# Three graph-attention layers: partly filled neighbour columns packed densely in all layers, their sources picked by one-hot products

## The chip, the cores and the metric

The kernel runs on one core of a Trainium2 chip. The metric is the device time of one execution in microseconds, the median of several runs. The engines are named as the profile names them: PE (matmul), DVE (vector), ACT (scalar), POOL (GpSimd, which issues the indirect DMAs here) and SP (which issues the plain DMAs).

## What is computed

A graph of 6250 nodes with 256 features and 100000 directed edges (`src`, `dst`, sorted by `dst`) goes through two GATv2 layers of 4 heads by 64 (with a self edge for every node), a residual and a layer norm, then one GAT layer of 8 heads by 32, a residual and a layer norm. Cut to what matters, one head of each kind of layer:

```python
# GATv2, twice (elu in between); edges include the self loops
xl, xr = x @ Wl, x @ Wr
logit = sum(att * leaky_relu(xl[src] + xr[dst], 0.2))
alpha = softmax of logit over the edges with the same dst
h[n]  = sum over edges with dst == n of alpha * xl[src]  + b
x = layernorm(x + h)
# GAT
Wh = x @ W
e  = leaky_relu(a1 . Wh[src] + a2 . Wh[dst], 0.2)
out[n] = sum of softmax(e) * Wh[src];  x = layernorm(x + out)
```

All arithmetic is in float32. An edge costs one gathered row of 256 numbers (1 KB) in each layer.

## The kernel before

**Plan.** `make_plan` sorts the nodes by degree on the chip and cuts them into 49 blocks of 128, one node to a partition, the fullest first. For each block it leaves in DRAM (`near_d`) a list of sources: column j holds the j-th neighbour of each of the 128 nodes, or a dummy node whose row makes the logit hugely negative. The number of columns of a block is fixed ahead from a model of the degrees (`columns`): 27 for block 0, 25 for block 1, then 24, 23, 22, down to 9 for block 48; 803 in all. The few edges of block 0 beyond 27 columns are handled apart (`find_few`). While DVE and PE work on the plan, POOL issues seven gathers whose result nobody reads (`spare`, L1259).

**Gathers.** `gather_rows` (L1475) fetches one column of one block with one indirect DMA of POOL: 128 rows, one to a partition. The last column of a block is often filled in a few nodes only. Ten such last columns are put into three packs of up to 128 lanes: `pick_rows` copies their list entries into one index column with small DMAs of SP, `gather_pack` (L1451) gathers the pack at once, and `lay_rows` and `lack_rows` (SP) put the lanes and the dummy rows into the block's rows tile. So a layer has 793 + 3 gathers of 128 rows. The lists of a pack's later blocks are fetched early for that, and layer 1 leaves the packs' indices for the other layers.

**Rows.** There are 9 rows tiles of 9 columns. A block's columns and the node's own row are cut into chunks that fit a tile: in layers 1 and 2 block 0 has four chunks, blocks 1 to 17 three, blocks 18 to 48 two.

**Layers 1 and 2** are `layer2(i, ...)`, called twice; all order is written by hand (`tc.manual_schedule`), and each engine runs its instructions in program order. One iteration b of the loop at its end:

- `attend(b)`: for each chunk z = max(g, pr), z times att, and a reduce to the logits (L1841, L1844, L1845, all DVE; the first z of a block is made one iteration ahead, in `first_z`, L1821); then the maximum `top` (L1623), ACT's exp, the denominators, and `first_z(b+1)`, which needs pr of that block (L1930 fills a part of pr first).
- `finish(b-1)`: elu, or residual and layer norm, of the block before.
- `weighted_sum(b)` (L1659): the rows times their weights, the last `few` columns by ACT (`mul`, L1673, four for each column), the others by DVE (L1677), and the sum over the columns in PSUM by PE with identity matmuls (`acc`, L1684). In layer 1 `few` is a third of the S columns, in layer 2 two thirds.
- `fetch(b+2)`: the list or rows of block b+4 (`begins`), the packs and the gathers of block b+2.
- `turns(b+2)`: PE transposes (`pt`), ACT copies to `xT`, PE makes pl and pr of block b+2 and the next layer's tables of block b-1, which SP stores as rows of `xl_d`, `xr_d` or `whs_d`.

PE does all of this in the order given: what fetch or turns issue stands behind the whole of acc(b).

**Layer 3** (L2022 on) has its own loop: gather(b+1), then attend(b) with one add per chunk for the logits (L2056), softmax, and `added_up`, products and one long reduce, all on DVE. PE is idle there.

Of the kernel before, what the change touches and what calls it, by code (L numbers as in the profile page):

```python
# [47 lines left out]
def columns(E, N, NB):  # L48
# [30 lines left out]
    part = {}  # L79
    for b in range(len(EARLY), NB):  # L80
        c = cols[b] - 1
        n = max(8, -(-int(math.ceil(over[c] + 3.5 * sd[c] - P * b)) // 8) * 8)
        if n < P:
            part[b] = n
    packs, taken = [], set()
    for b in sorted(part):
        if b in taken or part[b] > P * 3 // 4:
            continue
        pack, at = [], 0
        for k in range(b, NB):  # L90
            if k in part and k not in taken and at + part[k] <= P:
                pack.append((k, at, part[k]))
                at += part[k]
        if len(pack) > 1:
            packs.append(pack)
            taken.update(k for k, _, _ in pack)
    return cols, low, high, held, packs
# [569 lines left out]
def kernel(  # L667
# [22 lines left out]
    cols, low, high, held, packs = columns(E, N, NB)  # L690
# [7 lines left out]
    node_i = plan.tile([P, NB], I32, name="node_i")  # L698
    fits = plan.tile([P, 1], I32, name="fits")
# [11 lines left out]
    with tc.manual_schedule():  # L711
        make_plan(
            tc, x, src, dst, ((wl1, wr1, att1), (wl2, wr2, att2)), (b1, b2), w3, a3,
            cols, low, high, held, packs, node_i, fits, ident, eps, nobody, att, wc, wh, fixed, xl1_d,
            near_d,
        )
        nc.vector.memset(done, 0)
# [4 lines left out]
    with tc.If(ok != 0):  # L722
        with tc.manual_schedule():
            tile_by_degree(
                tc, x, att1, b1, b2, w3, a3, out, [held] + cols[1:], packs, node_i, near_d, ident, eps, nobody,
                xl1_d, att, wc, wh, fixed, done, wl2, wr2, att2,
            )
# [8 lines left out]
def make_plan(  # L736
    ctx, tc, x, src, dst, layers, biases, w3, a3, cols, low, high, held, packs, node_i, fits, ident, eps,
    nobody, att, wc, wh, fixed, xl1_d, near_d,
# [36 lines left out]
    SPARE = 7  # L775
# [218 lines left out]
    for pack in packs:  # L994
        for b, _, n in pack:
            nc.gpsimd.tensor_scalar(
                most[:, b : b + 1], part_of, float(n), float(cols[b] - 1), op0=OP.is_lt, op1=OP.add
            )
# [260 lines left out]
    spare = one.tile([P, SPARE, LONG], I32, name="spare")  # L1259
    for k in range(SPARE):  # L1260
        nc.gpsimd.indirect_dma_start(
            out=spare[:, k, :], out_offset=None, in_=listed,
            in_offset=bass.IndirectOffsetOnAxis(ap=begin_i[:, k : k + 1], axis=1),
        )
# [12 lines left out]
    counts = one.tile([P, NB], F32, name="counts")  # L1277
# [26 lines left out]
def tile_by_degree(  # L1304
    ctx, tc, x, att1, b1, b2, w3, a3, out, cols, packs, node_i, near_d, ident, eps, nobody,
    xl1_d, att, wc, wh, fixed, done, wl2, wr2, att2,
# [52 lines left out]
    late = consts.tile([P, len(EARLY)], F32, name="late")  # L1359
# [78 lines left out]
    packed = {b: (q, r, n) for q, pack in enumerate(packs) for b, r, n in pack}  # L1438
    opens = {pack[0][0]: q for q, pack in enumerate(packs)}
    shuts = {pack[-1][0]: q for q, pack in enumerate(packs)}  # L1440
    picks = [consts.tile([P, len(packs)], I32, name=f"pick{k}") for k in range(2)]
    for pick in picks:
        nc.gpsimd.memset(pick, NP)
    held_rows = {}

    def pick_rows(q, pick, of):

        for b, r, n in packs[q]:
            nc.sync.dma_start(pick[r : r + n, q : q + 1], of[:n, b, cols[b] - 1 : cols[b]])

    def gather_pack(b, pool, name, pick, table, width):  # L1451
        q = opens[b]
        held_rows[q] = pool.tile([P, RW], F32, name=name)
        nc.gpsimd.indirect_dma_start(
            out=held_rows[q][:, :width], out_offset=None, in_=table,
            in_offset=bass.IndirectOffsetOnAxis(ap=pick[:, q : q + 1], axis=0),
        )

    def lay_rows(b, rows, width):

        q, r, n = packed[b]
        nc.sync.dma_start(rows[-1][:n, rows_at[b], :width], held_rows[q][r : r + n, :width])

    rows_at = {}

    def lack_rows(b, rows, cut, table, width):

        n = packed[b][2]
        rows_at[b] = cut[-1][1] - cut[-1][0] - 1
        nc.sync.dma_start(  # L1470
            rows[-1][n:, rows_at[b], :width],
            bass.AP(tensor=table.tensor, offset=table.offset + NP * width, ap=[[0, P - n], [1, width]]),
        )

    def gather_rows(b, rows, cut, own, table, of, width, j0, j1):  # L1475


        for g, (s0, s1) in zip(rows, cut):
            for j in range(max(s0 - own, j0), min(s1 - own, j1)):
                if j + 1 == cols[b] and b in packed:  # L1480
                    continue
                nc.gpsimd.indirect_dma_start(  # L1482
                    out=g[:, j + own - s0, :width], out_offset=None, in_=table,
                    in_offset=source(of, b, j),
                )
# [84 lines left out]
    def sort_sources(work, ps, b):  # L1570

        n = cols[b]
# [19 lines left out]
        if b + 1 == len(EARLY):  # L1592
            pb = ps.tile([P, b + 1], F32, name="pb", tag="tp")
# [148 lines left out]
    def layer2(i, table, of, width, start, own, finish, follow):  # L1742
# [5 lines left out]
        with ExitStack() as es:  # L1748
# [5 lines left out]
            packp = es.enter_context(tc.tile_pool(name=f"pack{i}", bufs=len(packs)))  # L1754
# [5 lines left out]
            def gather(b):  # L1760
                first = EARLY[b] if b in begun else 0
                rows, cut = begun.pop(b) if first else row_tiles(b, 1)
                if b in opens:
                    gather_pack(b, packp, "pack", picks[i], table, width)
                gather_rows(b, rows, cut, 1, table, of, width, first, cols[b])
                if b in packed:
                    lack_rows(b, rows, cut, table, width)
                    if b in opens:
                        waiting.append(lambda: lay_rows(b, rows, width))
                    else:  # L1770
                        lay_rows(b, rows, width)
# [4 lines left out]
            waiting = []  # L1776
# [6 lines left out]
            def fetch(b):  # L1783
                if b + 2 < NB:
                    begins(b + 2)
                if i == 0 and b + 2 in opens:
                    for k, _, _ in packs[opens[b + 2]]:
                        begins(k)
                if i == 0 and b + 1 in opens:
                    pick_rows(opens[b + 1], picks[0], sources)  # L1790
# [35 lines left out]
            def attend(b):  # L1826
# [8 lines left out]
                for g, (s0, s1) in zip(rows, cut):  # L1835
# [11 lines left out]
                    )  # L1847
                if b == 0:
# [9 lines left out]
                few = min(S // 3, cut[-1][1] - cut[-1][0] - 1) if i == 0 else (2 * S - 2) // 3  # L1858
# [4 lines left out]
                if i == 0:  # L1863
# [3 lines left out]
                    if b in shuts:  # L1867
                        pick_rows(shuts[b], picks[1], spots)
# [15 lines left out]
            if i == 0:  # L1884
                find_few(work, pst)
            gather(0)
# [8 lines left out]
            for b in range(NB):  # L1895
# [6 lines left out]
                if b:  # L1902
                    new()

# [12 lines left out]
                if i == 0 and b == len(EARLY):  # L1917
                    load_last()
                if b + 2 < NB and not ahead(b):
# [102 lines left out]
    layer2(0, xl1_d[:, :], sources, W2 + 1, start1, own1, finish1, begin2)  # L2022
    last_weights()
    layer2(1, xl2_d[:, :], spots, W2, start2, own2, finish2, lambda: begin(0, wh_d, A1))

    with ExitStack() as es:
        packp = es.enter_context(tc.tile_pool(name="pack3", bufs=len(packs)))
        work = es.enter_context(tc.tile_pool(name="work3", bufs=3))
        ps = es.enter_context(tc.tile_pool(name="ps3", bufs=3, space=PSUM))
        state = {}  # L2030

        def gather(b):
            first = EARLY[b] if b in begun else 0
            rows, cut = begun.pop(b) if first else row_tiles(b, 0)
            if b in opens:
# [126 lines left out]
```

## Time and profile before

| | us |
|---|---|
| median of 9 runs | 3807.47 (3797.38 to 3831.42) |
| profiled execution | 3815.2 |
| its span | 3813.4 |
| DVE busy | 2720.6 (71%) |
| POOL busy | 2479.0 (65%) |
| PE busy | 1595.5 (42%) |
| ACT busy | 1330.7 (35%) |
| row gathers of layers 1 and 2, POOL (L1482) | 1549, 946 ns each |
| row gathers of layer 3, POOL (L1482) | 756, 1039 ns each |

One profiled execution gives busy times per engine, the idle time in front of each group of instructions and what ended it. The span is that of the instructions; the execution's own time is a little longer. In lines of waits the columns are the total, the number and the longest; in lines of the timeline they are start, duration, engine, line, operation, tiles out<-in, shape and count, with the idle time before the instruction and its releaser in brackets. "issue" is idle time for which the profile shows no cause.

### The profile page before, as it was taken

What the parts mean: (1) busy time and instruction counts of PE and PEld (TensorE: products, weight loads), DVE (VectorE), ACT (ScalarE), POOL (GpSimd) and SP (SyncE); (2) the same over time, 40 slices, a digit from 0 to 9 for tenths busy, and PEclk for the clock granted to TensorE, in tenths of its full rate; (3) what the DMA queues carried; (4) which work ended last, traced back from release to release, by engine and by line L of the source; (5) the groups of instructions that cost most, each with busy time, mean ns of one, the idle gap of its engine ahead of it and who ended that gap; (6) DMA issues with size and microseconds to landing.
All of it is one profiled execution on the core that took longest, in us unless ns stands there. A gap on an engine that the chain in (4) does not pass through costs nothing.

```text
span 3813.4 us, 25469 instructions
## 1 busy us (share of the span) xinstructions
PE 1595.5 (42%) x5424; PEld 1153.7 (30%) x5424; DVE 2720.6 (71%) x2619; ACT 1330.7 (35%) x5161; POOL 2479.0 (65%) x2585
## 2 busy tenths in 40 slices
PE   8235666566556774466655666664000000000000
PEld 6224454344445552343433444443000000000000
DVE  7638888667677886678866788894777566656665
ACT  3113434333334442456555667773000000000000
POOL 5764666665466655666666666664777777777774
PEclk9667888777778896788877778896555555555555
DMA  8433333333233433333433344442433333333332
GB/s 233 125 89 83 105 105 102 106 98 94 77 103 104 111 101 96 100 104 105 114 102 107 111 116 115 117 118 71 109 107 102 98 96 96 98 97 99 99 100 57
DMA packets 176463, 397.64 MB, mean 104 GB/s; under 512 B 50923, under 2 KB 93955, under 8 KB 176283
## 3 DMA queue, kind: packets, MB, share of 16 engines
q0 software_dynamic: 120608, 336.86, 32.5%
q1 hardware_dynamic: 54680, 57.74, 4.9%
q10 hardware_dynamic: 1012, 1.32, 0.1%
q8 instruction: 48, 0.79, 0.1%
q14 instruction: 115, 0.94, 0.1%
HBM read 354.60 MB, written 40.42 MB: 104 GB/s over the span
## 4 chain that ended last, share of the span: by engine, by line
POOL 16%; issue 16%; ACT 13%; DVE 7%; PE 6%; another core or an unknown queue 5%; DMA 1%; POOLq 0%; DVEq 0%; ACTq 0%
POOL g L1482 15%; ACT g L1673 9%; PE acc L1684 5%; ACT at L1631 1%; DVE weighted L1706 1%; DVE acc_v L1718 1%; POOL out L2086 1%; DVE z L1844 1%; DVE lg L1845 1%; PE pm L1612 1%; DVE part_v L1718 1%; DVE z L1841 1%; DMA g<-whs_d,near_r 1%; DVE g L1677 0%
## 5 line engine op out<-in xcount | busy, mean ns | idle before, releaser
L1482 POOL DMA_INDIRECT g<-xl_d,near_r x1549 | 1465.3, 946 | 826.2 <-issue 486.9
L1684 PE MATMUL acc<-g,ident 128*128 128x256 f32 x3408 | 1085.0, 472 | 807.6 <-issue 332.8
L1684 PEld LDWEIGHTS acc<-g,ident 128*128 128x128 f32 x3408 | 754.8, 234 | 1130.6 <-issue 402.5
L1482 POOL DMA_INDIRECT g<-whs_d,near_r x756 | 785.2, 1039 | 276.1 <-issue 244.5
L1673 ACT ACTIVATE g<-g,by 128x64 f32<-128x64 f32 x3080 | 796.4, 337 | 367.8 <-issue 350.7
L1845 DVE TENSOR_REDUCE lg<-z 128x28 f32<-128x1820 f32 (+4 forms) x234 | 497.4, 2125 | 8.1
L1844 DVE TENSOR_TENSOR z<-z,at 128x1820 f32<-128x1820 f32 (+4 forms) x234 | 496.8, 2123 | 4.7
L1718 DVE TENSOR_REDUCE acc_v<-weighted 128x256 f32<-128x3584 f32 (+10 forms) x47 | 319.0, 6787 | 22.3 <-remote 9.9
L1841 DVE TENSOR_TENSOR z<-g,pr 128x1820 f32<-128x1820 f32 (+3 forms) x138 | 299.6, 2171 | 16.9 <-DMA g<-xl_d,near_r 7.8
L1648 ACT ACTIVATE wt<-lg 128x128 f32<-128x128 f32 (+17 forms) x49 | 14.0, 285 | 801.9 <-DVE lg L1647 269.5
L1677 DVE TENSOR_TENSOR g<-g,at 128x256 f32<-128x256 f32 (+8 forms) x185 | 273.7, 1496 | 3.7 <-DVE at L1644 0.4
L1607 ACT COPY xT<-pt 128x256 f32<-128x256 f32 x147 | 51.8, 373 | 534.7 <-PE pt L1602 280.1
L1706 DVE TENSOR_TENSOR weighted<-g,wt 128x1792 f32<-128x1792 f32 (+4 forms) x111 | 227.1, 2057 | 0.3
L1821 DVE TENSOR_TENSOR z<-g,pr 128x2080 f32<-128x2080 f32 (+4 forms) x96 | 197.9, 2061 | 26.5 <-remote 13.8
L2056 DVE TENSOR_TENSOR lg<-g,s_r 128x56 f32<-128x56 f32 (+4 forms) x111 | 22.6, 213 | 268.3 <-DMA g<-whs_d,near_r 236.1
L1930 DVE MEMSET pr<- 128x4 f32 x49 | 3.0, 62 | 253.9 <-PE pr L1612 110.4
L1631 ACT ACTIVATE at<-lg,top 128x19 f32<-128x19 f32 (+14 forms) x392 | 115.8, 295 | 142.3 <-DVE top L1623 60.3
L1612 PE MATMUL pl<-wcat,xT 128*128 128x260 f32 x196 | 81.8, 559 | 90.5 <-ACT xT L1607 80.0
L1728 DVE BATCH_NORM_STATS2 stats<-acc 128x6 f32<-128x256 f32 x49 | 21.1, 430 | 130.4 <-PE acc L1684 84.7
L1612 PE MATMUL pm<-wcat,xT 128*128 128x260 f32 x392 | 102.7, 408 | 13.1 <-ACT xT L1607 13.1
L1612 PEld LDWEIGHTS pm<-wcat,xT 128*128 128x128 f32 x392 | 81.5, 209 | 28.8 <-ACT xT L1607 13.9
L1638 DVE RECIPROCAL den<-den 128x4 f32<-128x4 f32 x98 | 17.0, 174 | 99.5 <-ACT at L1631 61.1
(276 smaller groups left out, 1801.4 us busy)
## 6 DMA issues: line engine op xcount, KB each, us to landing
g<-xl_d,near_r POOLq DMA_INDIRECT x1549
g<-whs_d,near_r POOLq DMA_INDIRECT x756
whs_d<-row SPq DMA_DIRECT2D x49, 132.0 KB
xl_d<-row SPq DMA_DIRECT2D x49, 130.0 KB
xr_d<-row SPq DMA_DIRECT2D x49, 130.0 KB
two<-xl_d SPq DMA_DIRECT2D x49, 130.0 KB
two<-xr_d SPq DMA_DIRECT2D x49, 130.0 KB
near_d<-x_all SPq DMA_DIRECT2D x7, 896.0 KB
```

What stands on the lines that cost most here:

```text
L1482: nc.gpsimd.indirect_dma_start(out=g[:, j + own - s0, :width], out_offset=None, in_=table, in_offset=source(of, b, j),)
L1612: nc.tensor.matmul(pm, xT[:, c, :], w[:, c, :], start=c == 0, stop=c == 1)
L1631: nc.scalar.activation(wt[:, :, h], lg[:, :S, h], AF.Exp, bias=top[:, h : h + 1], accum_out=den[:, h : h + 1],)
L1673: nc.scalar.mul(g4[:, t, h, :], g4[:, t, h, :], by[:, s0 + t - a0, h : h + 1])
L1677: nc.vector.tensor_mul(g4[:, :m], g4[:, :m], wt[:, s0 : s0 + m, :].unsqueeze(3).to_broadcast([P, m, H, F // H]),)
L1684: nc.tensor.matmul(acc, ident, g4[:, t], start=False, stop=s0 + t == S - 1 and not more)
L1706: nc.vector.tensor_mul(prod[:, s0 - base : s1 - base, :].rearrange("p t (h d) -> p t h d", h=H), g[:, :n, :F].rearrange("p t (h d) -> p t ...
L1718: nc.vector.reduce_sum(part, prod[:, : s1 - base, :].rearrange("p s f -> p f s"), axis=AX.X)
L1821: nc.vector.tensor_max(z, rows[0][:, :n, :W2], xr[:, None, :].to_broadcast([P, n, W2]))
L1841: nc.vector.tensor_max(z, g[:, :n, :W2], xr[:, None, :].to_broadcast([P, n, W2]))
L1844: nc.vector.tensor_mul(z, z, at[:, None, :].to_broadcast([P, n, W2]))
L1845: nc.vector.reduce_sum(lg[:, s0:s1, :], z.rearrange("p t (h d) -> p t h d", h=H2), axis=AX.X)
```

## The change

`columns` no longer packs last columns only. `lanes_of` takes every column that by the model of the degrees is less than 75% filled: 33 columns in 28 of the blocks 1 to 48. All their edges, in the order of block, column and partition, are numbered through, and 128 in a row make a pack: 14 packs, dense to the last. The other 770 columns are gathered as before (`base[b]` of them in block b). Since the fill of a column is known only on the chip, the place at which a column begins in the packs is a value found at run time.

- `find_lanes`, at the start of layer 1: counts the edges of each such column (a compare with the nodes' degrees, a matmul with ones), sums them up, holds the sums within bounds fixed ahead (a breach leads to the slow path that is there for any graph), and leaves for every edge its pack and lane.
- `pick_lanes`: for each column a one-hot matrix of the lanes and one of packs times source; their product by PE, summed in PSUM over the columns at hand, gives the sources of the packs. It is called at the start of layer 1 (lists of blocks 0 to 2), in attend(0), and in layer 1's fetch whenever new lists were begun. The sum is added to `pick_f` by DVE after the first chunk of the next attend.
- `gather_packs`, `keep_packs`: a pack is gathered by POOL and stored to DRAM (`pack_d`). `lay_rows` loads each column from there into its place in the rows tile, from a row offset that SP loads into a register; partitions without an edge get some row, and `shut_lanes` adds a hugely negative number to their logits. `lack_rows` puts dummy rows where a column's upper partitions are never filled.
- `pick_again`, in layer 1: the packs' own indices for the other two layers come back from the stored rows' last column.
- The neighbour lists are begun earlier in layer 1, as far as the packs need them; the `spare` gathers, the old picks and packs are gone; in layer 1 `few` is two fifths of the columns; the pack tiles come from the pool `two` in layers 1 and 3.

The diff, cut to its core:

```diff
+    items, top, base = [], [], list(cols)
+    for b in range(1, NB):
+        size = min(P, N - P * b)
+        for c in range(low, cols[b]):
+            if min(size, over[c] - 3.5 * sd[c] - P * b) < 0.75 * P:
+                base[b] = min(base[b], c)
+                items.append((b, c))
+                top.append(max(8, min(P, -(-math.ceil(over[c] + 3.5 * sd[c] - P * b) // 8) * 8)))
...
-    spare = one.tile([P, SPARE, LONG], I32, name="spare")
-    for k in range(SPARE):
-        nc.gpsimd.indirect_dma_start(
...
+        for k, values in enumerate((lo, hi, [0] + top)):
+            i = 0
+            for j in range(1, len(values) + 1):
+                if j == len(values) or values[j] != values[i]:
+                    nc.vector.memset(bound[:, k, i:j], float(values[i]))
+                    i = j
+        for b, own in items_of.items():
+            nc.vector.tensor_scalar(
+                has[:, own[0] : own[-1] + 1], numbers[:, base[b] : cols[b]], counts[:, b : b + 1],
+                None, op0=OP.is_lt,
+            )
...
+        pk = ps.tile([P, K], F32, name="lane_k", tag="tp")
+        for i in range(first, written[0]):
...
+            hot_l = work.tile([P, P], F32, name="lane_hot", bufs=2)
+            nc.vector.tensor_scalar(hot_l, numbers, lane_in[:, 0, i : i + 1], None, op0=OP.is_equal)
+            given = work.tile([P, K], F32, name="lane_given", bufs=2)
+            nc.vector.tensor_scalar(
+                given, numbers[:, 1 : K + 1], lane_in[:, 1, i : i + 1], lane_in[:, 2, i : i + 1],
+                op0=OP.is_equal, op1=OP.mult,
+            )
+            nc.tensor.matmul(pk, hot_l, given, start=i == first, stop=i + 1 == written[0])
...
+        def add():
+            nc.vector.tensor_add(pick_f, pick_f, pk)
...
+    def keep_packs(b, k):
+        for q in packs_at.get(b, ()):
+            nc.sync.dma_start(pack_d[k][q * P : (q + 1) * P, :], held_rows[q][:, : wide[k]])
...
+            nc.sync.dma_start(g[: top[i], j - s0, : wide[k]], pack_d[k][lane(i), :])
...
+    def shut_lanes(b, lg, own, H):
+        if b in items_of:
...
+            nc.vector.tensor_add(s, s, shut[:, i0 : i0 + n].unsqueeze(2).to_broadcast([P, n, H]))
...
+                if i == 0 and b > 1:
+                    pick_lanes(work, pst, begun_lists[0])
+                gather_packs(b, pack_tile, picks[i], table, width)
+                keep_packs(b, i)
...
+                    while summed:
+                        summed.pop(0)()
...
-                few = min(S // 3, cut[-1][1] - cut[-1][0] - 1) if i == 0 else (2 * S - 2) // 3
+                shut_lanes(b, lg, 1, H2)
+                if i == 0 and b == 0:
+                    pick_lanes(work, pst, begun_lists[0])
+                few = min(2 * S // 5, cut[-1][1] - cut[-1][0] - 1) if i == 0 else (2 * S - 2) // 3
...
+                find_lanes(zp, pst)
+                pick_lanes(work, pst, 3)
+                summed.pop()()
             gather(0)
```

## The prediction

> **What bounds the kernel now.** First I read the page's busy shares and its slices.
>
> ```profile
> PE 1595.5 (42%) x5424; PEld 1153.7 (30%) x5424; DVE 2720.6 (71%) x2619; ACT 1330.7 (35%) x5161; POOL 2479.0 (65%) x2585
> DVE  7638888667677886678866788894777566656665
> POOL 5764666665466655666666666664777777777774
> PEclk9667888777778896788877778896555555555555
> ```
>
> No engine is full. A slice is 95 us: layer 1 takes slices 2 to 15 (98 to about 1473 us), layer 2 the next 12 (to 2650), layer 3 the rest. POOL, which issues every gather, is at 6 tenths in layers 1 and 2 and at 7 in layer 3. Its waits, in a stretch of layer 2 (1480 to 2100) and then in layer 3 (2900 to 3600), tell them apart:
>
> ```profile
> POOL g L1482 <- issue: 119.1, 391, 0.3
> POOL g L1482 <- PE acc L1684: 61.3, 19, 8.3
> POOL g L1482 <- remote: 32.2, 9, 4.7
> ```
> ```profile
> POOL g L1482 <- issue: 156.5, 461, 1.6
> ```
>
> The columns are us in total, times, longest. "issue" is the 0.30 us between two gathers: with 0.95 busy, a gather costs 1.25 us of POOL. In layer 2 POOL also stops once a block until PE's acc gives back a rows tile: it runs ahead of its users. In layer 3 it never waits for a tile. DVE's waits say the same, in layer 1 (300 to 700) and then in layer 3 (2660 to 3813):
>
> ```profile
> DVE pr L1930 <- PE pr L1612: 39.7, 9, 6.8
> ```
> ```profile
> DVE lg L2056 <- DMA g<-whs_d,near_r: 236.1, 31, 10.8
> ```
>
> In layer 1 DVE waits for pr, the end of a loop: DVE's weights and muls, ACT's muls, PE's acc, the transposes, pr, the next block's first z. In layer 3 it waits for the gathered rows. As a check I set each block's last gather against the start of DVE's last z of it. In layers 1 and 2, blocks 2 to 48, the gathers are done 24 to 74 us earlier; only blocks 0 and 1 are tight (9.8 and 5.3 us, then 4.6 and 16.7). In layer 3 blocks 9 to 43 end about 2 us behind the last gather, and blocks 44 to 48 are again 8 to 32 us ahead. So **only layer 3 is bound by gathers**, and its 756 row gathers take 785.2 + 276.1 us with their idle time, 1.40 us each (1.25 at best; I use 1.39, the pitch in 2900 to 3600).
>
> **The change, part by part.** The sum is against the profiled execution (3815.2 us, span 3813.4), which is 7.7 us, 0.2%, above the median of 3807.5; I carry the difference over to the median.
>
> *Fewer gathers.* By the degree model in the diff, 33 columns (28 blocks) go into 14 packs. A layer gathers 770 + 14 = 784 times against 793 + 3 = 796: 12 fewer. In layers 1 and 2 they end inside 24 to 74 us of lead: 0 (if that cover were not there, 24 x 1.25 = 30). In layer 3 the saving by block 42 is 8 gathers, 8 x 1.39 = 11.1; the last 4 fall where DVE is behind. What is late next is DVE, which waits only 4.9 and 3.3 us in blocks 41 and 42. Against it stand 28 adds of shut_lanes (0.2 us each, the nearest small op); about 5 lie in the DVE-bound tail, 1. **Layer 3: -10** (ends -17, all twelve, and 0, if lanes arrive late). A lane's chain there is a pack gather (0.95), its landing (2), the store and the load (2 to 3 each) and SP's register load (0.58 in this trace, 1.39 at worst): about 10 us, beside the block's own 8 to 20 gathers, 11 to 28 us.
>
> The Trainium skill's page "DMA: Bandwidth & Descriptors", section "Anatomy of one DMA — SWDGE (gpsimd) path", speaks against the change: it gives every DMA a fixed 2 us, most of it the write receipt, heaviest where HBM is written; a pack's trip through DRAM pays it three times in series. The row is the 2.0 to 2.2 us from last gather to first use; by the page the chain would be 6 us plus the loads, and as it lies beside the gathers the sum would be the same, or +6 for each block where it is not covered.
>
> *Idle gathers removed.* Seven of 1.18 + 0.3 us, 10.4 us of POOL between 30 and 70 us. POOL then waits for DVE:
>
> ```profile
> POOL near_d L1246 <- DVE moved L1243: 18.5, 2, 16.9
> ```
>
> They lie in front of a 16.9 us wait: 0 (ends -1 and +1). Ten small POOL ops on most go before the same wait: 0.
>
> *The old pick waits removed.* Between 900 and 1200 POOL stops twice at a pack:
>
> ```profile
> POOL pack L1454 <- DVE g L1677: 23.2, 1, 23.2
> POOL pack L1454 <- DMA pick<-near_r: 19.7, 1, 19.7
> ```
>
> Blocks 25 to 31 then still have 50 to 74 us of lead: 0 (end -43, both on the path).
>
> *The start of layer 1.* find_lanes stands on DVE before second_weights. Its memsets (85 runs of equal values in the bound tables, at the 0.062 us of DVE's small memset, 5.3), 28 compares at 0.17 (4.8), 16 small ops at 0.17 to 0.2 (3) and a matmul round (0.8, the wait at L1498) are 14 us. pick_lanes for four items adds four hot_l (0.28, as L1500), four given (0.2), three lane_in and a matmul round, 3.4. So 17 us go in ahead of this:
>
> ```profile
> 108.19 0.08 DVE L1389 MEMSET two<- 128x1 f32 x3
> 113.28 0.42 DVE L1403 TENSOR_TENSOR two<-two 128x256 f32<-128x256 f32 x1 [5.02 <-DMA two<-in_L_gnn_Wl]
> 120.58 0.06 DVE L1930 MEMSET pr<- 128x4 f32 x1 [4.69 <-DMA g<-xl_d,near_r]
> 128.42 2.05 DVE L1841 TENSOR_TENSOR z<-g,pr 128x1820 f32<-128x1820 f32 x1 [7.78 <-DMA g<-xl_d,near_r]
> ```
>
> The waits for gathered rows, and part of that for two, take up some 7; DVE then runs to 188 without a gap, so 10 go through. In attend(0) there are 10 more items, 10 x (0.28 + 0.2) + 9 x 0.17 + 1 for PE and the neighbour list, 7.3. The 17 lists that POOL now begins ahead of block 1's rows (17 x 1.25 = 21 us later) are covered by DVE's 39.5 us wait for block 0's acc. **Start: +17** (5 to 25; +21 more if that cover were gone).
>
> *The picks in layer 1.* This is the largest term. fetch issues, after block b's acc, the hot products; on PE they stand behind all of acc(b). The sum is added to pick_f by DVE in attend(b+1) after the first chunk's reduce, so DVE waits there for acc(b), and behind that add stand the other chunks of z, the maximum and the next first z. Fetch calls that pick are those of b = 1, 3, 5, 6, 13 (blocks of 3 chunks) and 17, 18, 23, 32 (2 chunks). For b = 13, DVE and then PE:
>
> ```profile
> 617.38 1.78 DVE L1845 TENSOR_REDUCE lg<-z 128x24 f32<-128x1560 f32 x1
> 630.88 0.28 DVE L1623 TENSOR_REDUCE top<-lg 128x4 f32<-128x76 f32 x1
> 636.04 0.06 DVE L1930 MEMSET pr<- 128x4 f32 x1 [4.88 <-PE pr L1612]
> ```
> ```profile
> 630.81 2.08 PE L1684 MATMUL acc<-g,ident 128*128 128x256 f32 x4 [3.51 <-remote]
> 632.68 0.64 PE L1602 MATMUL pt<-ident,near_r 128*128 128x128 f32 x2
> ```
>
> The first reduce ends at 619.2; acc ends at 632.7; the rest of the block's DVE work is 12.0 us. With the add, DVE goes on at about 633.9 and reaches the next first z at 646 instead of 636.3: 9.7 lost. The same working gives 0, 7.1, 10.3, 9.8, 9.7 for the 3-chunk calls and 4.0, 4.3, 4.1, 3.6 for the others. What waits for DVE is the whole loop (weights, then acc), so it adds up: **+53**. No end lies below nothing, as the adds take no work away. The low end, 15, holds if PE and ACT make up what DVE is late; the high end, 80, if the calls' own hot and given ops (23 items x 0.5) and a later acc come on top.
>
> *ACT's share.* few becomes 2S/5: 28 more columns in layer 1, in blocks from 18 on, 112 muls of 0.24 us from DVE (28 x 0.27 = 7.6) to ACT (27). ACT's muls run beside PE's acc in two paces, 0.24 and about 0.7 us each (L1673's 350.7 us of "issue"). I take **0**, as its gain and its loss lie on one loop; ends -8 and +78 (112 x 0.7).
>
> *Layer 2.* 28 shut_lanes (5.6 us) fall mostly into DVE's waits, here from 1480 to 2660:
>
> ```profile
> DVE stats L1728 <- PE acc L1684: 84.7, 27, 11.6
> DVE den L1638 <- ACT at L1631: 52.8, 32, 4.8
> ```
>
> 2 remain. Block 1's lane waits for packs gathered upon block 2: the 10 us chain inside 16.7 us of lead, 1. **+3** (0 to 10). On SP come 14 stores, 33 loads and 18 lack DMAs a layer, 14 small ones more in layer 1; a load that waits for its tile holds back the row stores behind it, whose readers are a layer away, and the x rows of two blocks later, which are issued before it: 0. Added bytes, 14 x 0.13 + 33 x 0.08 = 4.4 MB a layer, stand against 398 MB at a mean of 104 GB/s: 0. end_packs' three DMAs and ACT's one copy of picked come long before their first reader: 0. The hot sum shares the two PSUM tiles of pt and pm, and is given back by the add before the next pt: 0.
>
> **Sum**: -10 + 0 + 0 + 17 + 53 + 0 + 3 = +63, so 3878 profiled and **3870** against the median.
>
> **Rivals.** *POOL sets layers 1 and 2 after all.* Then DVE's waits are filled anyway, the picks cost 0, and 24 x 1.25 = 30, the two pack stops (43) and layer 3's 10 are all gained: -83 + 17 + 3 = -63, about **3745**. For it: DVE stands idle 20.1 us at 1009 and 17.5 at 1097, behind the pack stops. Against it: the lead of 50 us and more. It decides once the lead is under the 20 us of a stop.
>
> *The adds hide.* If the add costs its op alone, 17 + 3 + 5 - 10 = +15, less up to 8 from the moved muls: 3815, **no change**. For it: DVE waits 110.4 us for pr in layer 1 in any case. Against: the remaining chunks stand behind the add.
>
> *ACT's slow pace.* 112 muls at 0.7 us and not 0.24, on the loop: 63 + 78 = +141, **3948**. For it: DVE idle 29.9 us before 777 and 27.6 before 287, with ACT in that pace. Against: layer 2 gives ACT two thirds of the columns and runs no slower.
>
> **How the numbers follow.** Forecast 0.50, by itself 3830 to 3920 (the picks' 15 to 80, the start's 5 to 25); gathers bound 0.25; adds hidden 0.15; ACT slow 0.10. A measurement here tells about 0.5% (19 us) from no change. Faster by more: 0.26 (the gathers' case, a little of the hidden one). Same: 0.16. Slower: 0.58. The range leaves out the ACT case and the lower half of the gathers' case: 3760 to 3930.
>
> **What would show it.** Right: DVE adds on pick_f with waits of 5 to 14 us for the hot matmul at nine places in layer 1; layer 3's window shorter by about 10; the lead of layers 1 and 2 still over 20 us. Wrong: idle DVE at 1009 and 1097 gone with nothing in its place, or DVE waiting for gathers in layers 1 and 2, or no wait at the adds. What would make it wrong most easily is the pace of ACT's muls, which may shift by tens of us with any change of order.

## The result and the profile after

The changed kernel takes 3915.4 us (median of 14 runs, 3899.8 to 3929.6) against 3808.0 for the kernel before (46 runs): a ratio of 1.027, interval 1.025 to 1.029. Repeated on another chip it was 1.028 (1.023 to 1.034). The forecast was 3870, with a range of 3760 to 3930.

The profiled execution took 3908.6 us, its span is 3906.8, 93.4 longer than before. From the page of the changed kernel, busy shares and slices:

```profile
PE 1592.0 (41%) x5492; PEld 1166.6 (30%) x5492; DVE 2755.4 (71%) x2948; ACT 1367.5 (35%) x5274; POOL 2434.7 (62%) x2530
DVE  7166688865688686688776788897576666666655
POOL 3735566656554554566666666665677777777772
```

POOL is busy for 44 us less, as its 36 fewer gathers and the seven idle ones say; DVE and ACT are busy for 35 and 37 more. The second slice of DVE (98 to 195 us) is at 1 tenth, where it was at 6: that is the largest single loss, and the forecast had it small. Where the time went is read best from the start of the first z of each block (in layer 3, of the first logits), after minus before:

| mark | before, us | after minus before |
|---|---|---|
| layer 1, block 0 | 128.4 | +82.2 |
| block 3 | 288.0 | +61.9 |
| block 15 | 636.3 | +97.6 |
| block 25 | 920.6 | +106.9 |
| block 31 | 1110.9 | +78.5 |
| block 48 | 1418.1 | +116.1 |
| layer 3, block 0 | 2686.3 | +91.6 |
| layer 3, block 11 | 2957.9 | +100.9 |
| layer 3, block 33 | 3492.7 | +82.2 |
| layer 3, block 46 | 3755.9 | +96.8 |
| end of the span | 3813.4 | +93.4 |

**The start.** DVE's timeline of the changed kernel:

```profile
111.37 0.33 DVE L1487 MEMSET z<- 128x1 f32 x22
111.88 0.11 DVE L1487 MEMSET z<- 128x1 f32 x7 [0.18 <-issue]
114.73 0.13 DVE L1487 MEMSET z<- 128x1 f32 x8 [1.25 <-issue]
127.50 0.21 DVE L1490 TENSOR_SCALAR z<-numbers,counts 128x1 f32<-128x1 f32 x1 [0.49 <-issue]
128.90 0.33 DVE L1490 TENSOR_SCALAR z<-numbers,counts 128x1 f32<-128x1 f32 x2 [1.19 <-issue]
131.00 0.21 DVE L1490 TENSOR_SCALAR z<-numbers,counts 128x1 f32<-128x1 f32 x1 [1.07 <-issue]
156.23 0.18 DVE L1496 TENSOR_SCALAR lane_shut<-z 128x33 f32<-128x33 f32 x1 [9.59 <-remote]
177.23 0.19 DVE L1516 TENSOR_REDUCE late<-z 128x1 f32<-128x34 f32 x1 [1.20 <-DVE z L1515]
193.99 0.17 DVE L1557 TENSOR_TENSOR pick_f<-pick_f,lane_k 128x14 f32<-128x14 f32 x1 [4.88 <-issue]
210.59 2.05 DVE L1988 TENSOR_TENSOR z<-g,pr 128x1820 f32<-128x1820 f32 x1 [2.41 <-ACT few_own L1979]
```

The first 22 memsets of find_lanes take a third of a microsecond. From then on DVE starts its instructions at multiples of 0.70 us (127.50, 128.90, 131.00), whether they wait for anything or not, seven or eight small memsets or one or two compares at a time. find_lanes has 129 instructions on DVE in 66.0 us, and the sum of the first pick comes 16.8 later.

**The adds.** DVE's waits from 380 to 800, and one of the adds in the timeline:

```profile
DVE pick_f L1557 <- PE lane_k L1553: 28.3, 4, 11.6
```
```profile
707.93 1.78 DVE L1992 TENSOR_REDUCE lg<-z 128x24 f32<-128x1560 f32 x1
721.28 0.17 DVE L1557 TENSOR_TENSOR pick_f<-pick_f,lane_k 128x14 f32<-128x14 f32 x1 [11.57 <-PE lane_k L1553]
```

The second is the call of b = 13 that the forecast worked out: DVE stands 11.6 us behind acc, as it was to do. Over the kernel it is 45.2 us in 8 waits of 2.2 to 11.6.

**Gathers.** POOL's waits in layer 2 (1580 to 2200) and in layer 3 (3000 to 3700), and DVE's in layer 3 (2755 to 3907):

```profile
POOL g L1618 <- remote: 42.2, 12, 4.8
POOL g L1618 <- PE acc L1820: 38.2, 16, 5.6
```
```profile
POOL g L1618 <- issue: 149.4, 444, 0.9
```
```profile
DVE lg L2219 <- DMA g<-whs_d,near_r: 185.7, 24, 10.9
DVE den L2271 <- remote: 39.7, 16, 3.9
```

In layer 2 POOL still stops for tiles. In layer 3 DVE waits 50 us less for gathered rows (236.1 before), and yet the layer is 1.8 longer. None of DVE's waits is put down to a lane or a pack; those put down to "remote", a releaser that the profile doesn't name, leave it open (den's were 27.5 us before).

In layer 1 POOL has a new stop, in front of the packs' gathers, for the picks:

```profile
POOL two L1573 <- DVE pick L1559: 187.1, 9, 56.4
```

The forecast gave it no price. It makes no gathered rows late: with each block's last gather set against DVE's last z of it, as in the forecast, the gathers of blocks 2 to 48 end 27 to 66 us ahead in layer 1 and 28 to 54 in layer 2. (The packs' own rows are not in this.)

**The tail of layer 3.** Block 45 in the changed kernel, then in the kernel before:

```profile
3828.90 0.31 DVE L2219 TENSOR_TENSOR lg<-g,s_r 128x40 f32<-128x40 f32 x2
3829.71 0.17 DVE L1611 TENSOR_TENSOR lg<-lg,lane_shut 128x8 f32<-128x8 f32 x1 [0.50 <-issue]
3831.11 0.25 DVE L2224 SCALAR_TENSOR_TENSOR lg<-lg 128x88 f32<-128x88 f32 x1 [1.24 <-issue]
3833.21 0.31 DVE L1759 TENSOR_REDUCE top<-lg 128x8 f32<-128x88 f32 x1 [1.85 <-remote]
```
```profile
3734.92 0.31 DVE L2056 TENSOR_TENSOR lg<-g,s_r 128x40 f32<-128x40 f32 x2
3735.73 0.25 DVE L2060 SCALAR_TENSOR_TENSOR lg<-lg 128x88 f32<-128x88 f32 x1 [0.50 <-DVE lg L2056]
3736.43 0.31 DVE L1623 TENSOR_REDUCE top<-lg 128x8 f32<-128x88 f32 x1 [0.45 <-DVE lg L2060]
```

The same steps of 0.70 us: from the logits to the maximum it is now 4.31 us and was 1.51. shut_lanes costs 0.17 of work and here several steps.

As a measure of the steps I added up DVE's idle time over 0.3 us in front of instructions that wait for nothing but DVE itself. It is good to some 10%, as it depends on which waits are counted as ended: 111 us in the kernel before (46 in 2700 to 2960, 63 in 3640 to the end) and 239 in the changed one (62 in 100 to 200, 14 up to 420, 80 in 2800 to 3160, 82 in 3690 to the end).

### The profile page after: what moved, and what is told of

Its sections match the earlier page's. It is cut to its first block, busy times and chain, and to the rows that moved or that the text cites. A ratio compares the mean times of both kernels' runs of the same rounds, so it can differ in the third digit from the quotient of the medians.

```text
span 3906.8 us, 26743 instructions
## 1 busy us (share of the span) xinstructions
PE 1592.0 (41%) x5492; PEld 1166.6 (30%) x5492; DVE 2755.4 (71%) x2948; ACT 1367.5 (35%) x5274; POOL 2434.7 (62%) x2530
## 4 chain that ended last, share of the span: by engine, by line
issue 22%; POOL 19%; DVE 12%; ACT 11%; PE 9%; another core or an unknown queue 5%; DMA 3%; POOLq 0%; DVEq 0%; ACTq 0%
POOL g L1618 18%; ACT g L1809 8%; PE acc L1820 7%; DVE z L1991 3%; DVE lg L1992 2%; DVE z L1988 2%; DVE z L1968 2%; DMA g<-whs_d,near_r 1%; ACT at L1767 1%; POOL out L2250 1%; DMA g<-xl_d,near_r 1%; DVE g L1813 1%; PE pm L1748 1%; DVE weighted L1842 1%
## 5 line engine op out<-in xcount | busy, mean ns | idle before, releaser
L1618 POOL DMA_INDIRECT g<-xl_d,near_r x1503 | 1425.6, 948 | 773.7 <-issue 443.7
L1820 PEld LDWEIGHTS acc<-g,ident 128*128 128x128 f32 x3408 | 774.3, 239 | 1113.9 <-issue 384.6
L1809 ACT ACTIVATE g<-g,by 128x64 f32<-128x64 f32 x3192 | 833.7, 338 | 440.7 <-issue 419.3
L1618 POOL DMA_INDIRECT g<-whs_d,near_r x733 | 758.6, 1035 | 260.2 <-issue 227.6
L1854 DVE TENSOR_REDUCE acc_v<-weighted 128x256 f32<-128x3584 f32 (+10 forms) x47 | 319.0, 6787 | 29.4 <-remote 12.2
L1813 DVE TENSOR_TENSOR g<-g,at 128x256 f32<-128x256 f32 (+7 forms) x185 | 266.2, 1456 | 6.6 <-DVE at L1780 3.4
L1573 POOL DMA_INDIRECT two<-xl_d,pick x14 | 13.3, 946 | 194.8 <-DVE pick L1559 187.1
L1748 PE MATMUL pl<-wcat,xT 128*128 128x260 f32 x196 | 70.1, 490 | 125.2 <-ACT xT L1743 80.5
L2250 POOL DMA_INDIRECT out<-y,node_i x49 | 52.4, 1070 | 66.6 <-ACT y L1876 44.7
```

What stands on the lines that cost most here:

```text
L1618: nc.gpsimd.indirect_dma_start(out=g[:, j + own - s0, :width], out_offset=None, in_=table, in_offset=source(of, b, j),)
L1748: nc.tensor.matmul(pm, xT[:, c, :], w[:, c, :], start=c == 0, stop=c == 1)
L1809: nc.scalar.mul(g4[:, t, h, :], g4[:, t, h, :], by[:, s0 + t - a0, h : h + 1])
L1813: nc.vector.tensor_mul(g4[:, :m], g4[:, :m], wt[:, s0 : s0 + m, :].unsqueeze(3).to_broadcast([P, m, H, F // H]),)
L1820: nc.tensor.matmul(acc, ident, g4[:, t], start=False, stop=s0 + t == S - 1 and not more)
L1854: nc.vector.reduce_sum(part, prod[:, : s1 - base, :].rearrange("p s f -> p f s"), axis=AX.X)
```

## The experiments

Two kinds of chip took part, and a number can only be read beside the kernel before on the same chip: on three of the four chips that ran the experiments the kernel before took 3798 to 3824 us, on the fourth 3233.5, where the steps of 0.7 us are all but missing. Each run below is set against the kernel before on its own chip.

**The adds put later: late_add.**

```diff
-                    while summed:
-                        summed.pop(0)()
...
                     first_z(b + 1)
+                if b:
+                    while summed:
+                        summed.pop(0)()
```

> Only the place of the add changes: DVE adds the hot sum to pick_f behind the next block's first z, and no longer behind the first chunk's reduce. Theory (the adds hold up DVE): their 45 us of waits in the trace of the changed kernel fall to under 5, and the time goes from 3915 to about 3870. Rival (PE and ACT absorb what DVE is late): the waits go as well, but the time stays at 3905 to 3915.

Measured 4000.2 against 3798.2, ratio 1.055 (1.051 to 1.059), 202 us over its kernel before, where the changed kernel is 107 over: neither theory. The waits at the add went, and others came in their place. From PE's waits in layer 1 of this run (100 to 1700), and POOL's over the kernel:

```profile
PE pl L1748 <- issue: 153.7, 11, 46.4
PE pl L1748 <- ACT xT L1743: 145.8, 25, 47.0
PE pm L1748 <- ACT row L2116: 46.8, 8, 10.2
```
```profile
POOL two L1573 <- DVE den L1774: 175.4, 8, 39.4
```

The hot sum lies in one of the two PSUM tiles that the transposes and the next layer's tables also use, and it now holds it through most of an iteration (in the changed kernel the first two of these rows are 44.3 and 80.5 us). The packs' gathers, and the rows behind them on POOL, wait longer as well: with one wait for the picks and one for a sort it is 258 us, where the changed kernel has 187. That the tile is what costs is argued from these waits, not isolated. The run says that the add can't be put off, and leaves its price open.

**The start moved: lanes_later.** find_lanes and the first two picks follow block 0's weighted_sum on DVE; find_lanes' scratch lies in another tile.

```diff
-                find_lanes(zp, pst)
-                pick_lanes(work, pst, 3)
-                summed.pop()()
             gather(0)
...
-                if i == 0 and b == 0:
-                    pick_lanes(work, pst, begun_lists[0])
...
+                if i == 0 and b == 0:
+                    find_lanes(work, pst)
+                    pick_lanes(work, pst, begun_lists[0])
+                    summed.pop()()
```

> find_lanes and the first two calls of pick_lanes stand behind block 0's weighted_sum on DVE, where DVE had 39 us of waiting before the change, and no longer in front of block 0's z. Theory (the changed kernel's loss of 82 us at the first z is the time of these instructions on the path): block 0's first z starts at about 130 us and not at 211, and the time falls by 40 to 70, to 3845 to 3875. Rival (the delay comes with the changed queues of POOL and SP and not with these instructions): the first z stays at 180 us or later and the time at 3900 or more.

Measured 3885.6, ratio 1.0234 (1.0215 to 1.0253): 87 us over its kernel before, where the changed kernel is 107 over. So some 20 are gained, less than the 40 to 70 expected. The trace is that of the fastest of its six runs (3864.9), so its marks lie some 20 us too low by the end. Block 0's first z is at 124.2, 4 earlier than before. But block 1's rows, behind 17 neighbour lists on POOL, now show:

```profile
170.64 2.32 DVE L1968 TENSOR_TENSOR z<-g,pr 128x2080 f32<-128x2080 f32 x1 [18.24 <-DMA g<-xl_d,near_r]
```

So the 21 us of lists are covered only as long as DVE is late. By block 3 the loss is 19.1, and by block 8 it is 55.2: the part of layer 1 in which the picks' calls lie. find_lanes took 25.8 us here, with its steps ending at 199 us, ten after the last gather of block 1 (POOL issues none from 189 to 217):

```profile
198.41 0.06 DVE L1487 MEMSET row<- 128x1 f32 x1 [0.64 <-issue]
199.11 1.39 DVE L1487 MEMSET row<- 128x1 f32 x55 [0.64 <-issue]
```

**No gathers beside find_lanes: held.** POOL reads pick_f before it gathers block 0.

```diff
                 summed.pop()()
+                free = work.tile([P, 1], F32, name="free", bufs=1)
+                nc.gpsimd.tensor_scalar(free, pick_f[:, :1], 1.0, None, op0=OP.mult)
             gather(0)
```

> POOL waits for pick_f before it gathers block 0, so find_lanes and the first pick run with no gather under way. Theory A (DVE's steps of 0.7 us come from gathers in flight beside it): find_lanes and pick take under 25 us and not 83. Theory B (they do not depend on the gathers): still over 60 us. The time itself is longer by what POOL waits.

DVE's timeline of this run:

```profile
116.30 1.92 DVE L1487 MEMSET z<- 128x1 f32 x84
118.33 3.39 DVE L1490 TENSOR_SCALAR z<-numbers,counts 128x2 f32<-128x2 f32 x27
125.33 0.19 DVE L1516 TENSOR_REDUCE late<-z 128x1 f32<-128x34 f32 x1
128.36 0.17 DVE L1557 TENSOR_TENSOR pick_f<-pick_f,lane_k 128x14 f32<-128x14 f32 x1 [0.70 <-PE lane_k L1553]
```

The same 129 instructions take 9.2 us, and the pick 3.0. With 51 to 65 of POOL's indirect DMAs issued meanwhile they took 66.0, 91.7 (the repeat), 63.9 (few_third) and 64.6 (late_add). Theory A holds: on this kind of chip find_lanes is slow because gathers run beside it. The run takes away both their issue on POOL and their transfers, and doesn't tell which of the two it is. Though block 0's gathers begin only after the pick, its first z is 67 us earlier than in the changed kernel; 26 of these are left at block 3 and 11 at the end. The one time was 3897.4 (before: 3798.2).

**ACT's share: few_third.**

```diff
-                few = min(2 * S // 5, cut[-1][1] - cut[-1][0] - 1) if i == 0 else (2 * S - 2) // 3
+                few = min(S // 3, cut[-1][1] - cut[-1][0] - 1) if i == 0 else (2 * S - 2) // 3
```

> ACT's share of layer 1's columns goes back to a third. Theory (the moved muls are worth nothing): 3915, within 10. Rival (ACT's slow pace makes them cost): 3890 or less. A third one (they take work off DVE on the path): 3922 or more.

Measured 3912.0, ratio 1.031 (1.028 to 1.033), beside 1.027 (1.025 to 1.029) and 1.028 (1.023 to 1.034) of the changed kernel on other chips: the moved muls are worth nothing clear of the noise. The third theory isn't excluded either.

**The picks before acc: early.** On top of lanes_later; the hot sum has a slice of the tile `at` of its own.

```diff
+            pk = both[:, W2 + (CM + 1) * H2 :]
...
+                    if i == 0 and b:
+                        if s0 == 0:
+                            pick_lanes(work, pk, begun_lists[0])
+                        else:
+                            while summed:
+                                summed.pop(0)()
...
-                if i == 0 and b > 1:
-                    pick_lanes(work, pst, begun_lists[0])
```

> As lanes_later (3886), and the picks of layer 1 go ahead of acc: the hot products are made after a block's first chunk and added after its second, in a PSUM slice of their own. Theory (the adds wait for acc and cost about 45): no wait of over 2 us at the adds, and 3886 goes to 3830 to 3850. Rival (the loss of layer 1 between blocks 3 and 48, 49 us in the trace of lanes_later, comes from something else): 3870 or more.

This ran on the chip without steps: 3280.3 against 3233.5, ratio 1.014 (1.013 to 1.016). My edit was flawed: the tile that now holds the sum also holds `at`, and DVE's waits show that z times att waited for the product:

```profile
DVE z L1989 <- PE at L1552: 46.6, 7, 8.0
```

So it moved the wait and didn't remove it, and decides between neither theory. On this chip the change has another balance: beside nopacks (below, the same chip) early is 74.8 us late at block 17 of layer 1, 32.3 at the start of layer 3 and 12.2 at its last block.

**No packs: nopacks**, the kernel before with its three packs off.

```diff
-    packed = {b: (q, r, n) for q, pack in enumerate(packs) for b, r, n in pack}
-    opens = {pack[0][0]: q for q, pack in enumerate(packs)}
-    shuts = {pack[-1][0]: q for q, pack in enumerate(packs)}
+    packed, opens, shuts = {}, {}, {}
```

> The kernel before without its three packs: ten more gathers a layer less three, 7, all columns gathered in full, no pick waits on POOL. Theory of the prediction (the 43 us of pack waits are covered; layer 3 pays 7 x 1.39): 3808 + 10 = 3810 to 3820. Rival (the pack waits are on the path of layer 1): 3808 + 10 - 43 = 3765 to 3785.

On the chip without steps: 3263.9 against 3233.5, ratio 1.009 (1.007 to 1.011). 30 us for 21 gathers is 1.4 each: there each gather counts, in all three layers. The rows say the same: in this run a block's last gather ends only 2 to 9 us ahead of DVE's last z of it in layer 1, and 2 to 7 in layer 2 from block 9 on. POOL's waits over the kernel agree, with 29.6 us for tiles beside 674.5 of issue:

```profile
POOL g L1480 <- issue: 674.5, 2213, 0.4
POOL g L1480 <- PE acc L1682: 29.6, 91, 2.1
```

**More gathers: more12 and more3**, one column of blocks 12 to 47 twice.

```diff
+                if own == 1 and j + 2 == cols[b] and 12 <= b < 48:
+                    nc.gpsimd.indirect_dma_start(
+                        out=g[:, j + own - s0, :width], out_offset=None, in_=table,
+                        in_offset=source(of, b, j),
+                    )
```

> The kernel before with one column of each of blocks 12 to 47 gathered twice in layers 1 and 2: 72 more gathers. Theory (gathers there end 24 to 74 us before they are used): within 10 of 3808. Rival (POOL sets these layers): 72 x 1.25 = 90 more, 3898.

> The kernel before with one column of each of blocks 12 to 47 gathered twice in layer 3: 36 more gathers. Theory (layer 3 is bound by gathers up to block 43): 32 to 36 x 1.39, 44 to 50 more, 3852 to 3858. Rival (DVE is as much the bound there): 20 more or less.

On the same chip: 3476.4 (ratio 1.075) and 3353.9 (1.037), that is 243 for 72 gathers and 120 for 36: 3.4 and 3.3 each, not 1.25. The second gather writes where the first one does, and POOL waited for the first to land; of more12:

```profile
POOL g L1487 <- DMA g<-xl_d,near_r: 140.8, 62, 4.1
```

The price is therefore that of a POOL stop, and the runs say only that on this chip POOL's time is the kernel's time in every layer.

**Both kernels again, unchanged: before_again, after_again.**

> The kernel before, unchanged, for a trace on this chip. One of the chips so far showed DVE, ACT and PE instructions in steps of 0.7 us in stretches of the program (3798 for this kernel), another hardly any (3233). Theory (the steps are the chip's): on a chip with steps 3800, layer 1 of 1350 us, gathers of layers 1 and 2 ending 24 to 74 us before use; on a chip without 3233, layer 1 of about 1080, POOL without a wait for tiles. Rival (the two times come from the kernels of the submission): 3800 here whatever the steps.

> The changed kernel, unchanged. On a chip with steps: 2.7% slower again. On a chip without: find_lanes and the first pick take 17 to 25 us with gathers beside them (not 83), the first z comes about 17 later, the adds' waits still cost some 30 to 45 in layer 1, and the 36 fewer gathers give back up to 45 where POOL sets the pace: 3233 to 3270, 0 to 1.2% slower. Rival (find_lanes is slow because of the gathers beside it, on any chip): find_lanes over 60 us on either, and 2% slower or more.

This chip had steps: 3809.9 (one run) and 3914.3, ratio 1.028. The gathers of layers 1 and 2, blocks 2 to 48, again end ahead of DVE's last z, by 25 to 73 us in the kernel before and 27 to 67 in the changed one. DVE's long stepped stretches in layer 3 lie at the same places in the order of its instructions as in the first traces: from the 2859th and the 3765th of the kernel before, from the 3204th and the 4059th of the changed one. They belong to the program and the kind of chip, not to chance. What the changed kernel does on a chip without steps was not run.

**The add after the last chunk: add_last**, on top of lanes_later.

```diff
                     nc.vector.reduce_sum(
                         lg[:, s0:s1, :], z.rearrange("p t (h d) -> p t h d", h=H2), axis=AX.X
                     )
-                    while summed:
-                        summed.pop(0)()
+                while summed:
+                    summed.pop(0)()
```

> As lanes_later (ratio 1.0234 to before, 3886 on a chip with steps of 0.7 us), and the picks' sum is added after the last chunk's reduce of the next block, not after the first, so no z stands behind the wait for acc. Theory (the adds cost about 45 by holding back the remaining chunks): 3835 to 3855, ratio 1.010 to 1.015, and the steps at blocks 5 to 8 and 15 of some 8 us each are gone. Rival (DVE's lateness there is not what sets layer 1): 3880 or more, ratio over 1.021.

Measured 3929.1 against 3824.3, ratio 1.026 (1.022 to 1.030); lanes_later had 1.023. The gain did not come. DVE's waits at the add fell from 62.3 us (lanes_later) to 5.2, and 7.2 more that are put down to "remote". PE waits instead, in the first row 208.3 us and not 85.0:

```profile
PE pl L1748 <- ACT xT L1743: 208.3, 26, 50.1
PE pm L1748 <- DVE pick_f L1557: 25.7, 5, 10.5
```

A good part of that row lies at blocks 21, 26 and 35, at the gaps of 38 to 50 us that are described at the end of the next section. So neither place of the add behind the first chunk is better. That the adds' 45 us would be saved without them is not shown by a run.

**No packs, on a chip with steps: nopacks_again.**

> The kernel before with its three packs off, all 803 columns gathered in full. On the chip without steps it was 30 slower, 21 gathers at 1.4. On a chip with steps, theory of the prediction (the pack waits are covered): 3808 + 10, up to 3825. Rival (the two pack waits of 43 us are on the path of layer 1): 3770 to 3785, with the gain between blocks 26 and 31.

3828.6 against 3824.3, ratio 1.000 (0.998 to 1.002): 4 us more, nearer to the forecast's 10 than to the rival's gain. The marks against the kernel before (its first trace) show more: block 25 is at +29.5, block 26 at +4.0, block 29 at +2.1, block 30 at -2.6, block 31 at -17.3. So 45 us are gained at blocks 26, 30 and 31, behind the places where POOL in the kernel before waits at a pack, and they are lost again elsewhere: 30 ahead of block 26 and 19 in layer 2 (from its first z to layer 3's first logits). What these losses are isn't shown; the trace is that of the slowest of ten runs, 3847.5, 19 above their median. DVE's waits between 880 and 1130, before and then without packs:

```profile
DVE pr L1930 <- PE pr L1612: 34.0, 3, 20.1
DVE h L1956 <- ACT pos L1951: 32.9, 2, 17.5
```
```profile
DVE pr L1928 <- DMA g<-xl_d,near_r: 21.4, 5, 5.0
DVE pr L1928 <- PE pr L1610: 18.0, 2, 16.7
```

DVE's waits for pos are gone, and of one of 13.5 us for pr in front of block 26 3.6 are left. The longest, in front of block 27, is still there; in the kernel before and then without packs:

```profile
1008.98 0.06 DVE L1930 MEMSET pr<- 128x4 f32 x1 [20.05 <-PE pr L1612]
1009.71 0.06 DVE L1928 MEMSET pr<- 128x4 f32 x1 [16.75 <-PE pr L1610]
```

So these 20 us, which the forecast's first rival and its signs counted as standing behind a pack stop, don't come from the packs.

## Right and wrong, step by step

The sign and the range held, the range in part by luck. The sum of +63 became +107 (+93 in the trace), and its terms were off in both directions. In the trace the loss is 62 us by block 3 (the start), 34 more by block 18 (mostly the picks), and 40 net at five gaps in layer 1 that no term of the forecast had and whose cause is open. Then 23 are gained at blocks 30 and 31 and 17 in layer 2, both put at about 0, and layer 3 adds 2 where it was to give 10. Of the signs, the waits at the adds came mostly true (2 to 12 us in eight places, for 5 to 14 in nine), and so did the lead of over 20 us; layer 3's window didn't get shorter.

- **Start, forecast +17.** Wrong in size: +82 at block 0's first z, +62 left at block 3. The term that failed is "find_lanes ... 14 us". The work was sized well (9.2 us and 3.0 for the pick, in held); that DVE would do it at that pace beside 51 to 65 of POOL's gathers and lists was wrong. The trace of before had a hint: in layer 3's tail its dependent small operations stood at steps of 0.7 or 1.4, and I read them as chains of waits.
- **Lists begun early, covered.** Held in the changed kernel, where DVE was later still; in lanes_later, 18 us of them came out.
- **The picks, forecast +53.** The mechanism is there: 45.2 us of waits. At the marks two blocks after a call the loss grew by 7.5, 6.6, 2.7 and 7.9 for b = 3, 5, 6, 13 (forecast 7.1, 10.3, 9.8, 9.7) and by 3.3, 4.1 and 4.3 for b = 18, 23, 32 (4.3, 4.1, 3.6); the call of b = 17 is hidden by a stall of before that is gone. That is 36 of 49 for these seven. The loss moves by up to 12.5 at other marks as well (from block 5 to 6, where no such step was forecast), so the sizes are rough. Three runs could not take the waits away without others in their place.
- **The old pick waits, forecast 0.** Wrong at their place: without packs 45 us go at blocks 26, 30 and 31. In the changed kernel the loss falls by 9.0 at block 30 and 13.7 at 31. At 26 no gain is to be seen, as an open gap stands there (below), and the 20.2 gained at 27 are not the packs', as nopacks_again shows. The step that failed is "blocks 25 to 31 then still have 50 to 74 us of lead: 0": the rows had indeed landed well before DVE went on, but DVE waited there for ACT and PE, not for rows. How POOL's stop reached them isn't shown, and neither is a gain in the total: nopacks_again, with 21 more gathers, took the same time.
- **Fewer gathers in layers 1 and 2, forecast 0; layer 2, forecast +3.** The 0 stands on chips with steps: a lead of 27 us and more in the changed kernel leaves the gathers nothing to give. Layer 2, from its first z to layer 3's first logits, became 17 us shorter; but with the same gathers it was 22 shorter in the repeat, 11 in few_third and 2 longer in held. So these differences, and the 19 of nopacks_again, are not the price of gathers; what they are is open. On the chip without steps the gathers count. No run on a chip with steps changes the gathers alone.
- **Layer 3, forecast -10.** Its total is +1.8. From its start to block 33 the loss falls by 9.4, and 6 fewer gathers up to there, at 1.39, are 8.3: that part of the mechanism held. (Blocks 0 to 11 lose 9.3 in DVE's steps, but the rows are early there, and the gathers make it up.) Blocks 33 to 46 lose 14.6, again in DVE's stepped stretch, where from block 41 on the rows are 5 us and more ahead. The term that failed is shut_lanes at 0.2 us.
- **Lanes late; idle gathers; ACT's share.** No wait of DVE is put down to a lane (POOL waits once, 3.5 us, for a load from pack_d), so as far as the rows tell the chain through DRAM is covered. The 2 to 3 us each that the forecast gave a pack's store and load stand in no row. The Trainium skill's page "DMA: Bandwidth & Descriptors", section "Anatomy of one DMA — SWDGE (gpsimd) path", gives its fixed 2 us for DMAs that GpSimd issues; of a pack's three only the gather is one, and no run here measures the other two. For row gathers the trace agrees: in layer 3, blocks 13 to 39, the first use of a block's last gather comes 1.8 to 2.3 us behind it. The idle gathers were not tested alone. ACT's share is 0 within the noise, as forecast.
- **Left open.** Between blocks 19 and 35 the loss jumps by 41 at block 21, 12 at 26 and 33 at 35, and falls by 26 at 19 and 20 at 27: +40 in all. At these marks ACT's copy of xT starts about 20 us after PE's last recorded matmul. The changed kernel, its repeat, few_third, held and lanes_later show such gaps (16 to 27 us) at blocks 21, 26 and 35; the kernel before, its repeat and nopacks_again (19 to 22) at 19 and 27. The four traces of the chip without steps have no gap over 8 us. Their cause wasn't found, and together they are over a third of the loss.

## What to carry to other kernels

Price a burst of small instructions by the pace at which an engine starts them in the stretch where it will stand, beside the work that runs there, and not by the duration of one. A lead in a buffered stream shows that the reader isn't waiting for that stream; it says nothing of the reader's other waits, which a stop of the writer may still move: follow these one by one. And a wait for a tile of a small pool comes back on another engine when it is moved; before moving it, list what the tile's holder keeps others from.

## What I had not expected of the hardware

On most chips here engines start their instructions in steps of 0.7 us in certain stretches of the program: DVE for 129 instructions in 64 to 92 us beside gathers and in 9.2 without, ACT's muls at 0.24 us and then at 0.7 or 1.4. On one chip there were none to speak of (DVE's idle time of this kind at most 5 us, ACT's 2, against some 111 and 369 in the kernel before), and the same program took 3233 us and not 3800. The steps start after a run of quick instructions (22 memsets of find_lanes in the changed kernel, 16 in lanes_later), stay at the same place of the program from run to run, and in one run outlasted the last gather by ten microseconds; so the gathers bring them on, at the start of layer 1 at least, but what the engine waits for isn't shown.
